# Seven products of quarters for layer 1's attention output, and layer 2 in three stages

## The chip, the cores and the metric

The kernel runs on one core of a Trainium2 chip. The metric is the device time in microseconds (us) of one execution; lower is better. The engines are named as the profile names them: PE is TensorE's matrix multiply and PEld its weight load, DVE is VectorE, ACT is ScalarE, POOL is GpSimd, and SP is SyncE, which here only issues DMA transfers. ACTq and SPq are the instruction streams of ACT and SP where they issue transfers.

## The reference

Four layers follow each other on `x` of shape (8, 512, 32, 32), all in float32. Two of them matter here.

```python
# layer 1: attention over the 1024 positions of an image
q, k, v = Wq x, Wk x, Wv x            # 64, 64 and 512 channels
scores = q^T k                        # (1024, 1024)
attn = softmax(scores, axis=-1)
out = v attn^T + x                    # 512 channels
# layer 2: add a bias, upsample by 2 with a 12-tap filter in both directions,
# leaky ReLU times sqrt(2), downsample by 2 with a 12-tap filter
```

Layer 0 is a group norm, an attention of eight heads, three steps `h + 0.1 tanh(W h)` and a projection, with a residual. Layer 3 is a conditional convolution block whose 1x1, 3x3 and 1x1 weights are mixed from eight experts by a router, with a residual.

## The kernel before

The eight images `b` are processed one after another through layers 0, 1 and 2; then layer 3 runs over all images. Each image's layer 2 result waits in DRAM (`spilled`) until then. The instructions are written with a tile framework: it gives every instruction to the queue of the engine that the code names, decides the order within each queue from its own estimates, places tiles in buffers and sets the semaphores. Each engine works its queue in order, so an instruction that waits holds up all that stand behind it.

SBUF holds seven `big` buffers of 128 x 4096 float32, taken by whatever tile is alive: `x` of this and the next image, `v`, the exponentials, halos, upsampled tiles, results. PSUM has three pools of two: `ps_sc` gives pairs of banks, `ps_tp` and `ps_mm` give single banks of 128 x 512.

Most 512 x 512 matrix products are already computed as seven products of quarters (the Strassen-Winograd scheme) in place of eight: `product`, whose matmuls all stand in L412, with `quarter_sums` making four sums of quarters of the data beforehand and callbacks named `made` that combine the products as they come out of PSUM. When a `product` has `rows=True` its matmuls have 256 columns, otherwise 512.

Layer 1 (`layer1`) for an image: queries and keys; `values`, the `v` of 1024 positions x 512 channels, as a `product`; between its steps, `scores(t)` computes transposed scores, and ACT their exponentials into `eT[0]` and `eT[1]` (L715), each 1024 keys by 512 of the queries; DVE adds them up into `accs` (L720, L722). `totals(sh)` turns `acc` into sums over the keys with 8 matmuls of one column (L729), and `inv` holds their reciprocals. Then comes a loop over eight row blocks `ic` of 128 positions:

```python
            for jc in range(SC):
                nc.tensor.matmul(
                    ps, eT[sh][:, jc, ts(u, P)], v[:, jc, :],
                    start=(jc == 0), stop=(jc == SC - 1),
                )
```

Each block is transposed (L756), gets a bias added (L758), is accumulated over eight key blocks of 512 channels (the lines above, L762), is multiplied by `inv` and added (L768), and its four image rows are written to a padded image in DRAM, `ypad`, by four transfers that ACT issues (L770). One block later SP issues the loads of a halo tile, `halo.load(t)`: four transfers of 9 x 14 pixels each (L796), which read back what the neighbouring blocks wrote. `midway` puts the next image's channel statistics (L277) in the middle of the loop.

Layer 2 first upsamples all eight tiles (`layer2_up`): for each tile four matmuls with a halo (L826), each followed by the leaky ReLU `leak`, ACT making 0.2 times the value (L810) and DVE the larger of the two (L811). Then it downsamples everything (`layer2_down`): three ranges of output rows, each from its own upsampled tiles, for each of four channel chunks (L857), evicted by ACT and DVE (L871 to L877). The next image's group norm follows.

On ACT's queue the square root of the next image's group norm (L294, with a table load) stands between the row writes of layer 1 and the first leak.

Of the kernel before, what the change touches and what calls it, by code (L numbers as in the profile page):

```python
# [17 lines left out]
P = 128  # L18
# [15 lines left out]
NT = 8  # L34
# [18 lines left out]
def tile_sequence(ctx: ExitStack, tc: tile.TileContext, a: dict, out: bass.AP, shifted: bool):  # L53
# [215 lines left out]

    def channel_stats(b, x):  # L270

        stats = work.tile([P, C], F32, tag="y", name=f"stats_{b}", bufs=2)
        stats = stats[:, 0 : CC * 2 * 6].rearrange("p (c h s) -> p c h s", c=CC, h=2)
        mv = small.tile([P, CC, 2], F32, tag="mv", bufs=2, name=f"mv_{b}")
        for cc in range(CC):
            for h in range(2):
                nc.vector.bn_stats(stats[:, cc, h, :], x[:, cc, ts(h, HALF)])  # L277
            nc.vector.bn_aggr(mv[:, cc, :], stats[:, cc, :, :].rearrange("p h s -> p (h s)"))
        return mv
# [387 lines left out]
    def layer1(b, x, w, midway):  # L667

        qk = big_tile(f"qk1_{b}", [P, S + HALF])
        q, k = qk[:, 0:S], qk[:, S : S + HALF].rearrange("d (p j) -> d p j", j=P)  # L670

        rows = [slice(HD * r, HD * r + HD) for r in range(2)]
        t_x = quarter_sums(f"x_{b}", x)
        for sh in range(2):
            ps = bank(ps_tp, name=f"qk1_{b}_{sh}")
            project(ps, w["qk1"], 0, x, sh)
            keys = ps[HD:P, :].rearrange("d (p r j) -> d p r j", r=2, j=P)
            for r in range(2):
                dst = k[rows[r], 2 * sh : 2 * sh + 2, :]
                if r == 0:  # L680
                    nc.vector.tensor_scalar_add(q[rows[r], ts(sh, HALF)], ps[0:HD, :], qk1_b[0:HD, :])
                    nc.vector.tensor_scalar_add(dst, keys[:, :, r, :], qk1_b[HD:P, :])
                else:
                    nc.scalar.activation(
                        q[rows[r], ts(sh, HALF)], ps[0:HD, :], AF.Identity, bias=qk1_b[0:HD, :]
                    )
                    nc.scalar.activation(
                        dst, keys[:, :, r, :], AF.Identity, bias=qk1_b[HD:P, :]
                    )
        shift = None  # L690
        if shifted:
            shift = big_tile(f"shift_{b}", [P, S])
            row_shifts(
                f"{b}", [q[rows[r], :] for r in range(2)],
                [qk[rows[r], S : S + HALF] for r in range(2)],
                [shift[HD * r : HD * r + 1, :] for r in range(2)],
            )
        v = big_tile(f"v1_{b}", [P, SC, C])
        eT = [big_tile(f"eT_{b}_{sh}", [P, SC, HALF]) for sh in range(2)]
        if b == 0:  # L700
            layer2_constants()
        inv = small.tile([P, SC], F32, tag="inv1", bufs=2, name=f"inv1_{b}")
        accs = {}

        def scores(t):
            sh, p = divmod(t, SC // 2)
            at = ts(sh, HALF)
            pool = (ps_tp, ps_mm)[t % 2]
            ps = [bank(pool, f"scores1_{b}_{t}_{r}") for r in range(2)]
            scores_T(  # L710
                ps, [k[rows[r], p, :] for r in range(2)], [q[rows[r], at] for r in range(2)],
                shift and [shift[HD * r : HD * r + 1, at] for r in range(2)],
            )
            for r in range(2):
                nc.scalar.activation(eT[sh][:, 2 * p + r, :], ps[r], AF.Exp)  # L715
            e = eT[sh][:, 2 * p : 2 * p + 2, :].rearrange("j r i -> j (r i)")
            if p == 1:
                accs[sh] = sums(f"acc1_{b}_{sh}")
                first = eT[sh][:, 0:2, :].rearrange("j r i -> j (r i)")
                nc.vector.tensor_add(accs[sh], first, e)  # L720
            elif p > 1:
                nc.vector.tensor_add(accs[sh], accs[sh], e)  # L722

        def totals(sh):
            acc = accs.pop(sh)
            ps = bank(ps_tp, f"total1_{b}_{sh}")
            for u in range(4):
                for r in range(2):
                    nc.tensor.matmul(  # L729
                        ps[:, u : u + 1], acc[:, r * HALF + u * P : r * HALF + u * P + P],  # L730
                        ones[:, 0:1], start=(r == 0), stop=(r == 1),
                    )
            at = slice(4 * sh, 4 * sh + 4)
            nc.vector.reciprocal(inv[:, at], ps[:, 0:4])
            for r in range(2):
                nc.gpsimd.tensor_add(seen, seen, acc[:, ts(r, HALF)])  # L736
            nc.gpsimd.tensor_add(seen[:, 0:4], seen[:, 0:4], inv[:, at])

        values = product(f"v1_{b}", w["v1"], x, t_x, positions(f"v1_{b}", v), rows=True)
        for _ in range(2):  # L740
            next(values)
        for steps in ((0,), (1, 2), (3, 4), (5, 6), (7,)):
            for t in steps:
                scores(t)
            next(values)
            if 4 in steps:
                totals(0)
        all_of(values)
        if b + 1 < B:
            w["v"] = weight("v", b + 1)  # L750

        halo = Halo(b)
        for ic in range(SC):
            ps = bank(ps_tp, f"xT_{b}_{ic}")
            for cc in range(CC):
                nc.tensor.transpose(ps[:, ts(cc, P)], x[:, cc, ts(ic, P)], ident)  # L756
            y = work.tile([P, C], F32, tag="y", name=f"y_{b}_{ic}", bufs=2)
            nc.vector.tensor_add(y, ps, row_bias)  # L758
            ps = bank(name=f"av1_{b}_{ic}")
            sh, u = divmod(ic, 4)  # L760
            for jc in range(SC):
                nc.tensor.matmul(  # L762
                    ps, eT[sh][:, jc, ts(u, P)], v[:, jc, :],
                    start=(jc == 0), stop=(jc == SC - 1),
                )
            if ic == 1:
                totals(1)
            nc.vector.scalar_tensor_tensor(y, ps, inv[:, ic : ic + 1], y, ALU.mult, ALU.add)  # L768
            for r in range(4):
                nc.scalar.dma_start(  # L770
                    ypad[b % 2][4 * ic + r + 3, 3 : W + 3, :], y[W * r : W * r + W, :]
                )
            if ic:
                halo.load(ic - 1)
            if ic == 3:
                midway()
        halo.load(NT - 1)
        halo.load_last()
        return halo

    class Halo:

# [19 lines left out]
        def load_last(self):  # L802
            self.read(self.last, H, 3, 3, W)

    def layer2_up(b, halo):
        up = []

        def leak(dst, ps, name):
# [1 line left out]
            nc.scalar.mul(t, ps, 0.2 * SQRT2)  # L810
            nc.vector.scalar_tensor_tensor(dst, ps, SQRT2, t, ALU.mult, ALU.max)  # L811

        for t in range(NT):
            if t % 2 == 0:
                two = big_tile(f"up_{b}_{t // 2}", [P, 8, C])
            up.append(two[:, 4 * (t % 2) : 4 * (t % 2) + 4, :])
            for c in (0, 2):

                n = 2 * t + c // 2
                if n % 3 == 2:  # L820
                    ps = [bank(name=f"up_{b}_{t}_{c + i}") for i in range(2)]
                else:
                    pair = ps_sc.tile([P, S], F32, tag="scores", name=f"up_{b}_{t}_{c}")
                    ps = [pair[:, ts(i, HALF)] for i in range(2)]
# [4 lines left out]
                    )  # L829
                for i in range(2):  # L830
                    leak(up[t][:, c + i, :], ps[i], f"{b}_{t}_{c + i}")
        ps = bank(name=f"up_{b}_63")[0 : 2 * W, :]
        nc.tensor.matmul(ps, up63_op[0 : 3 * W, :], halo.last, start=True, stop=True)
        up63 = tmp(f"up63_{b}")[0 : 2 * W, :]
        leak(up63, ps, f"{b}_63")

        return up, up63

    def layer2_down(b, up, up63, freed=lambda t: None):

        z = big_tile(f"z_{b}", [P, CC, S])
        for first, last, ts_ in ((0, 13, (0, 1, 2)), (9, 21, (3, 4)), (17, 31, (5, 6, 7))):
            for cc in range(CC):
                zr = z[:, cc, :].rearrange("p (h w) -> p h w", w=W)
                ps = bank(name=f"dn_{b}_{cc}_{first}")
# [26 lines left out]
                else:  # L875
# [3 lines left out]
                    if b + 1 < B:  # L879
                        nc.sync.dma_start(spilled[b][ts(cc, P), :], z[:, cc, :])  # L880
            freed(ts_[-1])
        return z

    with tc.tile_pool(name=f"weights_{run}", bufs=1) as wpool:
# [10 lines left out]
        for b in range(B):  # L895
# [10 lines left out]
            halo = layer1(b, x, w, midway)  # L906
            if not last:
                norm = norm_factors(b + 1, *stats)
                layer2_down(b, *layer2_up(b, halo))

# [85 lines left out]
                )  # L998
        return wt

    up, up63 = layer2_up(B - 1, halo)
    z_next = load_z(0)
    load_experts("w2_0", 3 * P)

    def freed(t):
        if t == 2:
            load_experts("w2_1", 3 * P)
        elif t == 4:
            load_experts("w2_2", 3 * P)
        else:  # L1010
            load_experts("w3", C)

    z_last = layer2_down(B - 1, up, up63, freed)
    wt_next = mixed(0)
    route(B - 1, B)
    for b in range(B):
# [126 lines left out]
```

## Time and profile before

Three runs took 4014.0 to 4014.68 us, median 4014.32. The profiled execution spans 4013.4 us.

| what | us busy | instructions |
|---|---|---|
| PE | 3931.3 | 13990 |
| DVE | 2416.2 | 3376 |
| ACT | 1092.8 | 1491 |
| POOL | 458.0 | 343 |
| PE, layer 1 exponentials by values (L762) | 450.1 | 1024 |
| PE, layer 2 upsampling (L826) | 233.0 | 512 |
| PE, layer 2 downsampling (L857) | 235.8 | 2048 |
| PE, layer 1 totals (L729) | 29.6 | 256 |
| DVE, leaky ReLU (L811) | 171.1 | 264 |
| ACT, leaky ReLU (L810) | 147.6 | 264 |

Every float32 matmul appears as two MATMUL records. A row of a timeline gives the start of a group of like instructions, the time to the end of its last, engine, line, operation, the tiles written and read, shapes and count; in square brackets stands the idle time before it and what ended that. A row of a table by stage gives the stretch, its length, and the busy time of PE, PEld, DVE, ACT and POOL with counts in brackets, then the granted TensorE clock, the share of the DMA engines that was busy, and GB/s. In a row of costliest groups stand busy time, mean ns of one, and after the bar the idle time of the engine before them.

### The profile page before, as it was taken

What the parts mean: (1) busy time and instruction counts of PE and PEld (TensorE: products, weight loads), DVE (VectorE), ACT (ScalarE), POOL (GpSimd) and SP (SyncE); (2) the same over time, 40 slices, a digit from 0 to 9 for tenths busy, and PEclk for the clock granted to TensorE, in tenths of its full rate; (3) what the DMA queues carried; (4) which work ended last, traced back from release to release, by engine and by line L of the source; (5) the groups of instructions that cost most, each with busy time, mean ns of one, the idle gap of its engine ahead of it and who ended that gap; (6) DMA issues with size and microseconds to landing.
All of it is one profiled execution on the core that took longest, in us unless ns stands there. A gap on an engine that the chain in (4) does not pass through costs nothing.

```text
span 4013.4 us, 36677 instructions
## 1 busy us (share of the span) xinstructions
PE 3931.3 (98%) x13990; PEld 1898.7 (47%) x13990; DVE 2416.2 (60%) x3376; ACT 1092.8 (27%) x1491; POOL 458.0 (11%) x343
## 2 busy tenths in 40 slices
PE   8999999999999999999999999999999999999998
PEld 4345543455435463355434564355634554345543
DVE  4777448634676437754586346764377445764885
ACT  1421224112332214212242124322142122321332
POOL 5320003000120003100030002200030001301000
PEclk9999999999999999999999999999999999999999
DMA  5002310131101420032101310023200221004432
GB/s 186 19 25 86 108 55 1 54 106 62 37 0 58 124 76 1 2 106 95 56 1 58 121 45 35 1 76 106 77 1 29 93 82 56 1 0 127 152 145 87
DMA packets 83546, 255.77 MB, mean 64 GB/s; under 512 B 13206, under 2 KB 19366, under 8 KB 76576
## 3 DMA queue, kind: packets, MB, share of 16 engines
q1 hardware_dynamic: 68368, 223.11, 15.7%
q10 hardware_dynamic: 12288, 16.79, 1.6%
q0 software_dynamic: 2704, 13.42, 0.9%
q8 instruction: 112, 1.84, 0.2%
q14 instruction: 74, 0.61, 0.0%
HBM read 192.47 MB, written 60.81 MB: 63 GB/s over the span
## 4 chain that ended last, share of the span: by engine, by line
PE 89%; DVE 7%; ACT 3%; issue 1%; DMA 0%; ACTq 0%; SPq 0%; DVEq 0%
PE scores L263 13%; PE av L626 11%; PE av L762 11%; PE inl_X L412 6%; PE dn L857 6%; PE v_X L412 4%; PE inl_Y L412 4%; PE inl_A L412 3%; PE c L1035 3%; DVE up L811 3%; PE v_Y L412 3%; PE proj_X L412 2%; PE k_X L412 2%; PE q_X L412 2%; PE v_A L412 2%; ACT leak L810 2%
## 5 line engine op out<-in xcount | busy, mean ns | idle before, releaser
L611 ACT ACTIVATE e<-scores 128x1024 f32<-128x1024 f32 x512 | 497.3, 1022 | 583.1 <-PE scores L263 583.0
L617 DVE TENSOR_TENSOR acc<-acc,e 128x1024 f32<-128x1024 f32 x384 | 494.1, 1287 | 122.9 <-ACT e L611 102.5
L263 PE MATMUL scores<-q,k 64*128 64x512 f32 x2048 | 511.0, 616 | 6.0 <-DVE v L493 3.3
L626 PE MATMUL av<-e,v 128*64 128x512 f32 x2048 | 494.1, 604 | 0.0
L762 PE MATMUL av<-v,eT 128*128 128x512 f32 x1024 | 450.1, 592 | 0.0
L643 POOL TENSOR_TENSOR seen<-seen,acc 128x512 f32<-128x512 f32 x128 | 213.5, 1668 | 1586.3 <-DVE acc L617 1581.3
L263 PEld LDWEIGHTS scores<-q,k 64*128 64x128 f32 x2048 | 175.8, 186 | 333.2 <-ACT e L611 162.1
L762 PEld LDWEIGHTS av<-v,eT 128*128 128x128 f32 x1024 | 189.6, 190 | 214.3 <-issue 212.1
L626 PEld LDWEIGHTS av<-e,v 128*64 128x64 f32 x2048 | 124.8, 136 | 338.8 <-issue 336.5
L826 PE MATMUL up<-halo,up_op 126*128 126x512 f32 x512 | 233.0, 604 | 12.8 <-DVE up L811 12.5
L857 PE MATMUL dn<-dn_op,up 128*128 128x126 f32 (+5 forms) x2048 | 235.8, 275 | 0.0
L857 PEld LDWEIGHTS dn<-dn_op,up 128*128 128x128 f32 (+1 forms) x2048 | 231.1, 192 | 8.7 <-DVE up L811 6.5
L768 DVE SCALAR_TENSOR_TENSOR y<-av,inv,y 128x512 f32<-128x512 f32 x64 | 48.0, 750 | 300.4 <-PE av L762 300.4
L640 DVE RECIPROCAL inv<-total 128x512 f32<-128x512 f32 x64 | 214.7, 3355 | 0.0
L811 DVE SCALAR_TENSOR_TENSOR up<-up,leak 128x512 f32<-128x512 f32 (+1 forms) x264 | 171.1, 685 | 62.2 <-ACT leak L810 56.6
L412 PE MATMUL inl_A<-hf,w_inl 128*128 128x512 f32 x384 | 178.0, 599 | 10.7 <-DVE hf L641 10.7
L412 PE MATMUL inl_X<-T_hf,w_inl 128*128 128x512 f32 x384 | 175.2, 592 | 0.0
L643 POOL TENSOR_TENSOR seen<-seen,inv 128x512 f32<-128x512 f32 x64 | 125.2, 1956 | 416.7 <-DVE inv L640 416.7
L810 ACT ACTIVATE leak<-up 128x512 f32<-128x512 f32 (+1 forms) x264 | 147.6, 594 | 88.3 <-DVE up L811 79.8
L826 PEld LDWEIGHTS up<-halo,up_op 126*128 126x128 f32 x512 | 91.9, 189 | 141.2 <-DVE up L811 74.3
L736 POOL TENSOR_TENSOR seen<-seen,acc 128x512 f32<-128x512 f32 x32 | 40.7, 1271 | 959.8 <-DVE acc L722 893.2
L506 ACT ACTIVATE inl_U<-inl_U,inl_b 128x512 f32<-128x512 f32 x96 | 66.7, 718 | 287.4 <-DVE inl_U L521 287.4
(273 smaller groups left out, 4986.9 us busy)
## 6 DMA issues: line engine op xcount, KB each, us to landing
halo<-ypad_u SPq DMA_DIRECT2D x256, 252.0 KB
w_v<-stored_u_v SPq DMA_DIRECT2D x14, 1792.0 KB
x<-in_x_dram SPq DMA_DIRECT2D x32, 512.0 KB
ypad_u<-y ACTq DMA_DIRECT2D x256, 64.0 KB
out_dram<-z SPq DMA_DIRECT2D x32, 512.0 KB
spill_u<-z SPq DMA_DIRECT2D x28, 512.0 KB
z<-spill_u SPq DMA_DIRECT2D x28, 512.0 KB
w_q<-stored_u_q SPq DMA_DIRECT2D x7, 1792.0 KB
```

Of the source, the lines that this page charges most:

```text
L263: nc.tensor.matmul(ps[r], k[r], q[r], start=True, stop=(shift is None))
L412: nc.tensor.matmul(dst, lhs, rhs, start=(opens and s == 0 and cc == 0), stop=(cc == 1 and s == rows), skip_group_check=True,)
L611: nc.scalar.activation(e, ps, AF.Exp, scale=HD ** -0.5)
L617: nc.vector.tensor_add(accs[g], accs[g], e)
L626: nc.tensor.matmul(avs[g][rows[r]], v[:, jc, ts(2 * oc + r, HD)], e[:, ts(r, HALF)], start=(jc == 0), stop=(jc == SC - 1),)
L640: nc.vector.reciprocal(inv, ps)
L643: nc.gpsimd.tensor_add(seen, seen, part)
L762: nc.tensor.matmul(ps, eT[sh][:, jc, ts(u, P)], v[:, jc, :], start=(jc == 0), stop=(jc == SC - 1),)
L810: nc.scalar.mul(t, ps, 0.2 * SQRT2)
L811: nc.vector.scalar_tensor_tensor(dst, ps, SQRT2, t, ALU.mult, ALU.max)
L826: nc.tensor.matmul(ps[i], up_op[0 : IR * IC, :], halo.tile(t)[0 : IR * IC, c + i, :], start=True, stop=True,)
L857: nc.tensor.matmul(rows[:, r0 - first : r1 + 1 - first, c0 : c1 + 1], up[t][0:k, c, ts(cc, P)], op[:, r0 - 4 * t + 3 : r1 + 4 - 4 * t, c0 ...
```

## The change

Layer 1's product of exponentials by values, 1024 x 1024 by 1024 x 512, is itself split into quarters and computed with seven products in place of eight (`weighted_rows`), to take an eighth of its matmul work away. The sums of quarters that this needs are made by DVE from the exponentials and from `v`: S1 to S4 of 512 x 512, T1 to T4 of 512 x 256. All matmuls now have 256 columns (L855 of the new kernel). A block of rows is complete only quarter by quarter: in the order C11, C12 (the upper rows), C22, C21 (the lower rows). So each image row is written by two transfers of half size (L765), and all transposes with the bias come first, into a big tile `y`.

The extra big tiles leave fewer buffers, so layer 2 is interleaved: upsample tiles 0 to 2, downsample the first range of rows, upsample 3 and 4, downsample the second, upsample 5 to 7, downsample the third. Its odd PSUM pairs come from `ps_tp` in place of `ps_mm`. In the last image the loads of the expert weights of layer 3 move to later points. `totals` first adds the halves of `acc` on DVE, so that four matmuls are enough, and the statistics take their scratch from the `sums` tiles.

```diff
         def totals(sh):
             acc = accs.pop(sh)
+            both = acc[:, 0:HALF]
+            nc.vector.tensor_add(both, both, acc[:, HALF:S])
             ps = bank(ps_tp, f"total1_{b}_{sh}")
             for u in range(4):
-                for r in range(2):
-                    nc.tensor.matmul(
-                        ps[:, u : u + 1], acc[:, r * HALF + u * P : r * HALF + u * P + P],
-                        ones[:, 0:1], start=(r == 0), stop=(r == 1),
-                    )
+                nc.tensor.matmul(
+                    ps[:, u : u + 1], both[:, ts(u, P)], ones[:, 0:1], start=True, stop=True
+                )
...
-        halo = Halo(b)
+        y = big_tile(f"y_{b}", [P, SC, C])
         for ic in range(SC):
             ps = bank(ps_tp, f"xT_{b}_{ic}")
             for cc in range(CC):
                 nc.tensor.transpose(ps[:, ts(cc, P)], x[:, cc, ts(ic, P)], ident)
-            y = work.tile([P, C], F32, tag="y", name=f"y_{b}_{ic}", bufs=2)
-            nc.vector.tensor_add(y, ps, row_bias)
...
+            nc.vector.tensor_add(y[:, ic, :], ps, row_bias)
+        totals(1)
...
+        def write(ic, cols):
             for r in range(4):
                 nc.scalar.dma_start(
-                    ypad[b % 2][4 * ic + r + 3, 3 : W + 3, :], y[W * r : W * r + W, :]
-                )
...
+                    ypad[b % 2][4 * ic + r + 3, 3 : W + 3, cols], y[W * r : W * r + W, ic, cols]
+                )
+        def written(what, u):
+            for ic in (2 * u, 2 * u + 1):
+                if what == "C11":
+                    write(ic, slice(0, QR))
+                elif what == "C12":
+                    write(ic, slice(QR, C))
+                elif what == "C22":
+                    write(ic + 4, slice(QR, C))
+                elif what == "C21":
+                    write(ic + 4, slice(0, QR))
+            if what == "C12":
+                for t in ((0,), (1, 2))[u]:
+                    halo.load(t)
...
+        weighted_rows(b, eT, v, inv, y, written)
+        for t in range(3, NT):
+            halo.load(t)
         halo.load_last()
...
+    def weighted_rows(b, eT, v, inv, y, written):
...
+        by_two(add, s1, a21, a22)
+        by_two(sub, t1, b12, b11)
+        by_two(sub, s2, s1, a11)
+        by_two(sub, t2, b22, t1)
+        by_two(sub, s3, a11, a21)
+        by_two(sub, t3, b22, b12)
+        for what, key, left, right in (
+            ("P1", "A", a11, b11), ("C11", "A", a12, b21), ("U2", "X", s2, t2),
+            ("W", "Y", s1, t1), ("C12", "Y", s4, b22), ("C22", "X", s3, t3),
+            ("C21", "X", a22, t4),
+        ):
+            for u in range(2):
+                ps = banks[key][u]
+                for s in range(2):
+                    for j in range(4):
...
+                made(what, u, ps)
+                written(what, u)
+            if what == "C11":
+                by_two(sub, s4, a12, s2)
+                by_two(sub, t4, b21, t2)
...
+        for t in range(3):
+            upsample(t)
+        z = big_tile(f"z_{b}", [P, CC, S])
+        downsample(0, 13, (0, 1, 2))
+        for t in (3, 4):
+            upsample(t)
+        downsample(9, 21, (3, 4))
+        for t in (5, 6, 7):
+            upsample(t)
```

In the changed program as built, the matmuls, sums and transfers of one image interleave more finely than the code is written: two of the first upsampling matmuls stand among C21's, and on ACT's queue all 64 row writes of an image stand in one run.

## The prediction

> **What bounds the kernel now.** First the page's busy shares and its chain of waits: TensorE is busy 98% of the span and carries 89% of the chain, at full clock throughout, so a change is worth the TensorE time that it removes, less the TensorE waits that it makes.
>
> ```profile
> PE 3931.3 (98%) x13990; PEld 1898.7 (47%) x13990; DVE 2416.2 (60%) x3376; ACT 1092.8 (27%) x1491; POOL 458.0 (11%) x343
> PE 89%; DVE 7%; ACT 3%; issue 1%; DMA 0%; ACTq 0%; SPq 0%; DVEq 0%
> L762 PE MATMUL av<-v,eT 128*128 128x512 f32 x1024 | 450.1, 592 | 0.0
> L826 PE MATMUL up<-halo,up_op 126*128 126x512 f32 x512 | 233.0, 604 | 12.8 <-DVE up L811 12.5
> ```
>
> Then TensorE's timeline of the second image around the change. In it a group's length overlaps the next group's start, so I take differences of starts.
>
> ```profile
> 543.16 7.07 PE L412 MATMUL v_A<-w_v,h 128*128 128x256 f32 x32
> 550.07 2.11 PE L412 MATMUL v_X<-w_v,T_h 128*128 128x256 f32 x9
> ...
> 845.24 0.60 PE L756 MATMUL xT<-ident,x 128*128 128x128 f32 x4
> 845.68 7.03 PE L762 MATMUL av<-v,eT 128*128 128x512 f32 x16
> 852.55 1.84 PE L729 MATMUL total<-ones,acc 128*128 128x1 f32 x16
> 854.25 0.63 PE L756 MATMUL xT<-ident,x 128*128 128x128 f32 x4
> ...
> 905.40 23.33 PE L826 MATMUL up<-halo,up_op 126*128 126x512 f32 x52 [1.52 <-DVE up L811]
> 929.23 1.07 PE L833 MATMUL up<-halo,up_op 96*64 96x512 f32 x2 [0.50 <-DVE up L811]
> ```
>
> A 512-column matmul is two records: 16 in 852.55-845.68 = 6.87 us, 0.4294 each. With 256 columns 32 take 550.07-543.16 = 6.91, 0.2159 each. The totals take 1.70. The same image by stage, exponentials by values, then upsampling, then downsampling:
>
> ```profile
> 837.93:898.12 60.19, 60.19 (x178) 29.28 (x177) 16.97 (x30) 0.00 (x0) 1.80 (x3) 1.00 0.51 157
> 898.12:930.23 32.11, 30.09 (x72) 12.12 (x70) 21.45 (x40) 18.87 (x33) 0.00 (x0) 1.00 0.30 92
> 930.23:960.98 30.75, 30.75 (x266) 30.06 (x265) 16.61 (x29) 4.48 (x9) 0.00 (x0) 1.00 0.13 52
> ```
>
> The first stage is all TensorE. The second has 66 upsampling records, 28.3 us, and two small ones, 0.3; it lasts 32.1, so it loses 3.5 us an image. ScalarE's timeline and VectorE's say why:
>
> ```profile
> 899.10 1.74 ACTq L770 DMA_DIRECT2D ypad_u<-y  x4
> 901.15 1.28 ACT L294 ACT_TABLE_LOAD   x1 [65.59 <-DMA ypad_u<-y]
> 902.45 0.26 ACT L294 ACTIVATE gmul<-gn_var,eps 128x4 f32<-128x4 f32 x1
> 902.61 0.59 ACT L810 ACTIVATE leak<-up 128x512 f32<-128x512 f32 x1
> 904.02 1.08 ACT L810 ACTIVATE leak<-up 128x512 f32<-128x512 f32 x2 [0.82 <-DVE gadd L299]
> ...
> 911.93 2.70 DVE L811 SCALAR_TENSOR_TENSOR up<-up,leak 128x512 f32<-128x512 f32 x4 [0.66 <-ACT leak L810]
> ```
>
> ScalarE issues the row writes itself, 0.43 us each and 0.475 from one to the next, and only then loads its table and starts the leaks. The first leak starts 4.5 us after the last av matmul; leaks then go at 6 in 5.3 us, and twelve take from 902.61 to about 914.0 = 11.4. The reader should keep this line of four writes in mind.
>
> **What the skill says.** "TensorE: Matmul & The Clock Gate", Back-to-back issue gap, gives 262 cycles for 256 columns and 518 for 512: half the columns cost half the time. The trace agrees (0.2159 against 0.4294), so a seventh product less is a real eighth. "DMA: Bandwidth & Descriptors", Issuing engines are not separate DMA queues, says that issues from several engines share the same 16 DMA engines; its Anatomy of one DMA says that a semaphore wait is served by the issuing sequencer before dispatch. The first agrees with DMA share 0.51 in the stage of writes and loads; of the second the trace of before has no clear case, since only four writes come at a time.
>
> **The change, part by part, per image.**
> Products: 64 blocks of 512 columns (128 records x 0.4294 = 55.0) become 7 x 16 of 256 (224 x 0.2159 = 48.4): -6.6 us. Both totals halved: half of 1.70 and of 1.77, -1.7; the added VectorE addition of 128x512 (0.68) ends before TensorE arrives, for the v1 product lies between. Together -8.3, or -66 us for eight images.
>
> VectorE gets 8 half quarters of S of 1024 (1.2 us each) and 8 of T of 512 (0.68), and more evictions (no row has 256 columns with two inputs; between 0.32 for 160 and 0.68 for 512, I take 0.4). From the first transpose to the end of C12's first half TensorE has 8 x 0.43 + 0.85 + 78 x 0.432 = 38 us; the queued VectorE work there, with the next image's statistics (5.6), adds to about 28. Walked in queue order, S2 and T2 are ready 13 us after the first transpose and first read at 19; S4 and T4 at 21, read at 35. Hidden behind P1, C11 and U2. Only the moved transposes wait, for two PSUM banks that VectorE drains between sums: +0.7 (0 to 2).
>
> Row writes: 64 of half size in place of 32. Each still has 32 rows, so I keep 0.475 an issue. After C11's and C12's first half 40 are left, and in the changed program's instruction order all stand on ScalarE ahead of the table load and every leak. Let T be TensorE's end of C12's first half. Rows are ready at T+1.2 (0.2 to start, 0.61, 0.4); 48 writes take 22.8, to T+24.0 at best. TensorE meanwhile needs 18 blocks for C22 and C12, 16 for C21, two upsampling matmuls: it ends C21 at T+17 (with 0.4 of wait for the first halo load, which I put at T+8.2: 5.1 us from row to last packet in before, and four more writes ahead of it, 1.9). ScalarE, idle in before, is now late.
>
> Semaphores: in the built order every DMA of both queues waits for one of eight semaphores in turn, so for the DMA eight before it. Twelve halo loads (tiles 0 to 2) stand among the writes of C12 and C22, and four of tile 3 among C21's. Loads land one per about 1.1 us (252 KB each; the packets of nine take 9.3 us in before) after T+8.2, the twelfth near T+20; the writes behind wait for it. Then 14 writes, 6.7, and again a wait for tile 3's loads: T+29 (24 to 32). Plus 0.3, 1.3 and 0.2: first leak at T+30.5.
>
> Three stages: the first upsampling stage has 12 leaks, 11.4 us, and 0.5 for the last blocks: T+42.4. TensorE can do between T+17 and there only ten upsampling matmuls (8.6) and 24 downsampling blocks (x 0.23 = 5.4), 14.0. Wait: 42.4-17-14.0 = 11.4 us. The second stage's leaks fit beside the downsampling; the third, where the normalisation (4 x 0.75 on VectorE) joins, +1.0. What the three stages win is before's 3.5, which is gone.
>
> Sum: -8.3 - 3.5 + 11.4 + 0.7 + 0.4 + 1.0 = +1.7 us an image, +14 for eight: 4028. The last image also loads its expert weights later; by their order they land before their mixing is needed: nothing, up to +3.
>
> **The rivals.**
> A: the semaphores cost nothing and only issuing counts. Leak at T+25.7, wait 6.6, -3.1 an image: 3989. For it: no DMA wait shows in before. Against: in before writes and loads never interleave.
> B: ScalarE's queue is never the limit (half-size writes are issued in half the time). Then the waits stay as in before, 3.5, and 66 us come off: 3948. Against: a 32-row write and a 126-row load are issued in 0.43 and 0.79 us, so time goes with rows, not bytes.
> C: writes and loads press on the DMA engines harder (each load 1.3 us among writes): ScalarE done at T+32, wait 14.6, +4.9 an image: 4053, and more if VectorE's sums delay a product.
>
> **How the numbers follow.** My forecast 0.50, A 0.24, B 0.10, C 0.16. Faster: B, nine tenths of A and a little of the forecast, 0.36; same: 0.14 from the forecast's and A's edges; slower: 0.50. The low end, 3975, lies below A and leaves out B; the high end, 4062, takes in C with 1.1 us an image more for the unknown VectorE costs.
>
> **What would show it.** Right: under the new L855 TensorE about 390 us of busy time; the row writes in one unbroken run on ScalarE's queue that ends over 10 us after C21's last matmul; TensorE idle 6 to 14 us an image, ended by VectorE's up; the table load behind a DMA. Wrong: leaks that start within 5 us of C21's end (B); TensorE idle inside L855, ended by VectorE (sums late); idle ended by a halo DMA.

## The result, and the profile after

The changed kernel takes 4078.22 us (median; 4076.54 to 4080.41), the kernel before beside it 4014.5: ratio 1.0159, 95% interval 1.0142 to 1.0177. It is slower by 64 us, 8.0 us an image; the forecast was slower by 14, 1.7 an image. The page of the changed kernel:

```profile
PE 3890.1 (95%) x14630; PEld 2042.5 (50%) x14630; DVE 2587.0 (63%) x3664; ACT 1103.6 (27%) x1507; POOL 444.8 (11%) x327
PE 87%; DMA 5%; DVE 5%; ACT 1%; issue 1%; ACTq 1%; SPq 0%; DVEq 0%
L913 PE MATMUL up<-halo,up_op 126*128 126x512 f32 x512 | 256.2, 636 | 99.5 <-ACT gmul L295 92.3
L934 PE MATMUL dn<-dn_op,up 128*128 128x126 f32 (+5 forms) x2048 | 248.8, 277 | 16.8 <-DVE up L898 16.1
```

TensorE is busy 41 us less (3931.3 before), yet its share fell from 98% to 95%. DMA, which carried 0% of the chain of waits, carries 5%, some 200 us of span. The upsampling row names the place: its idle time ahead of it went from 12.8 to 99.5 us, 92.3 of that ended by `gmul`, the square root that stands on ScalarE's queue between the row writes and the leaks. TensorE's timeline of the second image:

```profile
845.49 1.04 PE L757 MATMUL xT<-ident,x 128*128 128x128 f32 x8
...
880.92 3.72 PE L855 MATMUL av_Y<-v,eT 128*128 128x256 f32 x16
884.47 1.03 PE L855 MATMUL av_X<-v,eT 128*128 128x256 f32 x4
...
894.48 1.10 PE L913 MATMUL up<-halo,up_op 126*128 126x512 f32 x2 [1.76 <-DMA halo<-ypad_u]
...
903.40 2.93 PE L913 MATMUL up<-halo,up_op 126*128 126x512 f32 x6
920.20 2.08 PE L913 MATMUL up<-halo,up_op 126*128 126x512 f32 x2 [13.87 <-ACT gmul L295]
...
978.49 6.71 PE L413 MATMUL q_A<-h,w_q 128*128 128x512 f32 x15
```

The first half of C12 ends at 884.47, which is the T of the prediction; C21 ends at 903.40 = T+18.9 (forecast T+17). Then TensorE does three upsampling matmuls and waits 13.9 us. From the first transpose to the next image's `q_A` it is 133.00 us; before it was 960.98-837.93 = 123.05. ScalarE's timeline shows what is waited for:

```profile
885.92 32.64 ACTq L765 DMA_DIRECT2D ypad_u<-y  x48
918.59 1.28 ACT L295 ACT_TABLE_LOAD   x1 [60.47 <-DMA ypad_u<-y]
919.88 0.26 ACT L295 ACTIVATE gmul<-gn_var,eps 128x4 f32<-128x4 f32 x1
920.04 0.59 ACT L897 ACTIVATE leak<-up 128x512 f32<-128x512 f32 x1
```

Before, this run had four writes (899.10, 1.74 us) and the first leak came 4.5 us after the last av matmul. Now it has 48, takes 32.64 us, and the first leak comes at T+35.6, 16.6 us after C21. At 0.475 an issue 48 writes are 22.8 us; the other 9.8 are waits inside the run. The forecast had T+30.5.

### The profile page after: what moved, and what is told of

Read it like the earlier page. It is cut to its first block, busy times and chain, and to the rows that moved or that the text cites. A ratio compares the mean times of both kernels' runs of the same rounds, so it can differ in the third digit from the quotient of the medians.

```text
span 4074.7 us, 38294 instructions
## 1 busy us (share of the span) xinstructions
PE 3890.1 (95%) x14630; PEld 2042.5 (50%) x14630; DVE 2587.0 (63%) x3664; ACT 1103.6 (27%) x1507; POOL 444.8 (11%) x327
## 4 chain that ended last, share of the span: by engine, by line
PE 87%; DMA 5%; DVE 5%; ACT 1%; issue 1%; ACTq 1%; SPq 0%; DVEq 0%
PE scores L263 13%; PE av L627 11%; PE inl_X L413 6%; PE dn L934 6%; PE up L913 5%; PE v_X L413 4%; PE inl_Y L413 4%; PE inl_A L413 3%; DMA halo<-ypad_u 3%; PE c L1129 3%; PE v_Y L413 3%; PE av_Y L855 2%; PE av_A L855 2%; PE proj_X L413 2%; PE q_X L413 2%; PE k_X L413 2%
## 5 line engine op out<-in xcount | busy, mean ns | idle before, releaser
L644 POOL TENSOR_TENSOR seen<-seen,acc 128x512 f32<-128x512 f32 x128 | 213.6, 1669 | 1681.7 <-DVE acc L618 1676.7
L913 PE MATMUL up<-halo,up_op 126*128 126x512 f32 x512 | 256.2, 636 | 99.5 <-ACT gmul L295 92.3
L934 PEld LDWEIGHTS dn<-dn_op,up 128*128 128x128 f32 (+1 forms) x2048 | 246.6, 194 | 67.5 <-issue 31.6
L934 PE MATMUL dn<-dn_op,up 128*128 128x126 f32 (+5 forms) x2048 | 248.8, 277 | 16.8 <-DVE up L898 16.1
L913 PEld LDWEIGHTS up<-halo,up_op 126*128 126x128 f32 x512 | 95.2, 200 | 193.2 <-ACT gmul L295 98.1
L616 DVE TENSOR_TENSOR acc<-e,e 128x1024 f32<-128x1024 f32 x64 | 82.9, 1295 | 102.5 <-ACT e L612 102.5
L518 DVE TENSOR_TENSOR inl_U<-inl_X,inl_P 128x512 f32<-128x512 f32 x96 | 61.9, 686 | 111.4 <-PE inl_X L413 111.4
L736 POOL TENSOR_TENSOR seen<-seen,acc 128x512 f32<-128x512 f32 x16 | 22.5, 1408 | 976.7 <-DVE acc L728 905.4
L413 PEld LDWEIGHTS inl_A<-hf,w_inl 128*128 128x128 f32 x384 | 70.4, 190 | 110.2 <-issue 95.4
```

Source lines behind the costliest of these rows:

```text
L413: nc.tensor.matmul(dst, lhs, rhs, start=(opens and s == 0 and cc == 0), stop=(cc == 1 and s == rows), skip_group_check=True,)
L644: nc.gpsimd.tensor_add(seen, seen, part)
L913: nc.tensor.matmul(ps[i], up_op[0 : IR * IC, :], halo.tile(t)[0 : IR * IC, c + i, :], start=True, stop=True,)
L934: nc.tensor.matmul(rows[:, r0 - first : r1 + 1 - first, c0 : c1 + 1], up[t][0:k, c, ts(cc, P)], op[:, r0 - 4 * t + 3 : r1 + 4 - 4 * t, c0 ...
```

## The experiments

All times are medians, against the kernel before on the same chip (4014.5 to 4015.2). They come in four groups: the parts alone, the row writes, a second wait behind the first, and TensorE's clock. Where an edit adds or takes away lines, the line numbers of its run shift by a few (L909 or L912 for L913).

### The parts alone

The halved totals, put into the kernel before (the first hunk of the change, nothing else):

> The kernel before with the halved totals alone (both totals: one VectorE addition and four small matmuls in place of eight). Theory: 8 x 1.7 us are saved, since TensorE has no slack there: 4001, 3998 to 4005. Rival (the added VectorE addition of 0.68 us is waited for, or the small matmuls overlap others): 4011 to 4016.

Measured: 3998.68 (ratio 0.9960, 0.9947 to 0.9974), 15.9 us less, a little more than the 13.6 forecast. TensorE's waits are as before: none took the place of the removed matmuls.

The kernel before with the totals and with layer 2 in three stages (with the banks and the later loads of the last image that belong to them), its av matmuls and row writes left as they were; the line that calls them:

```diff
-                layer2_down(b, *layer2_up(b, halo))
+                layer2(b, halo)
```

> The kernel before with the halved totals and layer 2 in three stages, but with its own products and row writes of 512 columns after each row block. Theory (three stages turn before's 3.5 us of TensorE waits in upsampling into a wait of 1 to 3 us for the first twelve leaks): 0 to 2.5 us an image less than with the totals alone, 3979 to 3999. Rival (the three stages themselves make the long wait, by asking for leaks earlier): over 4010.

Measured: 3981.69 (0.9917, 0.9900 to 0.9933), another 17.0 us: 1.6 us in each of the first seven images, and about 5 in the last, where the loads moved too. So three stages do not make a wait by themselves: two of the change's three parts together are 33 us faster than the kernel before, and what turns that into 64 slower is the new product with its row writes. The opposite cut, the changed kernel without three stages:

```diff
-        for t in range(3):
+        for t in range(NT):
             upsample(t)
...
         downsample(0, 13, (0, 1, 2))
-        for t in (3, 4):
-            upsample(t)
         downsample(9, 21, (3, 4))
-        for t in (5, 6, 7):
-            upsample(t)
...
         downsample(17, 31, (5, 6, 7))
```

> The changed kernel with all upsampling ahead of all downsampling, as before the change. Theory: 33 leaks at 0.95 us follow one another from 35.6 us after C12's first half, TensorE idles through them, then 30.75 us of downsampling: 97.7 us after it in place of 94.0, so 3 to 5 us an image more, 4100 to 4118. Rival (the three stages make the long wait): at most 4078.

Measured: 4077.77, no difference from the changed kernel. The expectation missed. The number is the rival's, but the three stages do not make the wait: without them TensorE still waits 11.8 us at layer 2's start in the second image, ended by `gmul`. From the first leak (921.23) to the next `q_A` (979.54) of the second image this kernel takes 58.3 us, the changed one 978.49-920.04 = 58.4, where I had worked out 33 x 0.95 + 30.75 = 62.1: some downsampling goes between the leaks here too. Where leaks start this late, the three stages gain nothing.

### The row writes

The writes moved to another queue:

```diff
         def write(ic, cols):
             for r in range(4):
-                nc.scalar.dma_start(
+                nc.sync.dma_start(
```

> The 64 row writes an image are issued on SyncE's queue instead of ScalarE's; all else as in the changed kernel. Theory (ScalarE's queue of writes holds the table load and the leaks back): the first leak no longer starts 35.6 us after C12's first half but within about 3 us of C21's end or of the landing of the first three tiles, TensorE's idle at layer 2's start falls from 14 to under 4 us an image, 11 to 16 us an image are saved: 3950 to 3990. Rival (the transfers are late whoever issues them: 24 writes at 0.475 and 12 loads at 0.83 on one queue still take over 21 us): the idle stays over 8 us, now ended by a halo DMA, and the time stays over 4030.

Measured: 4045.19 (1.0073, 1.0058 to 1.0088), 33 us better than the changed kernel, and short of the 88 to 128 expected. In its second image C21 ends at 899.70. ScalarE's first leak, and VectorE's half of the eighth and ninth leak:

```profile
900.82 0.60 ACT L897 ACTIVATE leak<-up 128x512 f32<-128x512 f32 x1 [5.07 <-PE up L913]
```

```profile
908.54 0.69 DVE L898 SCALAR_TENSOR_TENSOR up<-up,leak 128x512 f32<-128x512 f32 x1 [0.67 <-ACT leak L897]
919.52 0.69 DVE L898 SCALAR_TENSOR_TENSOR up<-up,leak 128x512 f32<-128x512 f32 x1 [10.29 <-DMA ypad_u<-y]
```

The first half of the theory holds: with the writes off its queue ScalarE starts 1.1 us after C21 instead of 16.6. Then VectorE stops at the ninth leak for 10.3 us, behind a row write. The ninth leak is the first of tile 2; its output `up_1` is a big tile of its own, and it was placed in the buffer of `y`, which is free only when the last row write has read it. In the other images the trace names a halo load as the end of this wait (64.6 us in six of them); on SyncE's queue writes and loads use the same eight semaphores in turn. The prediction had not seen this second wait.

The same bytes in half as many writes, on ScalarE's queue:

```diff
-                if what == "C11":
-                    write(ic, slice(0, QR))
-                elif what == "C12":
-                    write(ic, slice(QR, C))
+                if what == "C12":
+                    write(ic, slice(0, C))
...
                 elif what == "C21":
-                    write(ic + 4, slice(0, QR))
+                    write(ic + 4, slice(0, C))
```

> Each image row is written once with all its 512 columns, upper rows after C12 and lower rows after C21: 32 writes an image of 64 KB in place of 64 of 32 KB, the same bytes, on ScalarE's queue as in the changed kernel. Theory (the number of issues counts, not the bytes): the last write is issued about 24 to 30 us after C12's first half instead of 34, the first leak comes 4 to 8 us earlier, 32 to 64 us in all: 4014 to 4046. Rival (bytes or landings count): an issue takes twice as long and the time stays within 10 us of 4078.

Measured: 4033.91 (1.0049, 1.0034 to 1.0064), 44 us better. C12's first half ends at 883.00 in its second image and the table load starts at 910.56, so T+27.6 instead of T+34.1:

```profile
884.44 26.09 ACTq L765 DMA_DIRECT2D ypad_u<-y  x32
```

An issue of 32 rows takes the median 0.43 us whether a row has 1 KB or 2: the number of issues counts. Sixteen fewer are 7.6 us; the waits inside the run stay, 26.09 - 32 x 0.475 = 10.9 us. The Trainium skill agrees: "DMA: Bandwidth & Descriptors", Rules for kernel authors, says to coalesce many small transfers.

The halo loads of tiles 0 to 3 taken off the eight semaphores that they share with the writes:

```diff
-            nc.sync.dma_start(dst, pixels)
+            queue = nc.gpsimd if row <= 12 else nc.sync
+            queue.dma_start(dst, pixels)
```

> The halo loads of tiles 0 to 3 are issued on GpSimd's queue instead of SyncE's; the writes stay on ScalarE's queue. In the built order the writes then no longer share their eight semaphores with those loads. Theory (9.8 us of the 32.6 us run of writes are waits for loads that stand eight places before): the run of the last 48 writes shrinks to about 23 to 25 us, the first leak comes 8 us earlier, 40 to 70 us less: 4008 to 4038, unless GpSimd issues the loads so slowly that TensorE waits for them instead. Rival (the writes are slow because the DMA engines are busy): the run stays near 32 us and the time at 4078 or more.

Measured: 4059.01 (1.0106, 1.0090 to 1.0121), 19 us better; 40 to 70 were expected. The end of C12's first half (TensorE's timeline, the start of the group after it) and the table load (ScalarE's):

```profile
886.79 1.03 PE L855 MATMUL av_X<-v,eT 128*128 128x256 f32 x4
```

```profile
917.97 1.28 ACT L295 ACT_TABLE_LOAD   x1 [57.53 <-DMA ypad_u<-y]
```

That is T+31.2. Of the 9.8 us of waits in the run, taking these loads off the shared semaphores saves about 3. The other 7 remain when a write waits only for earlier writes: the write itself lands late. The DMA engines are busy 0.72 to 0.96 of the time around 912 to 920 in the changed kernel. In both kernels the writes follow each other without a gap until the loads have begun (loads from 890.78 and first gap over 0.1 us at 894.13 in the changed kernel, 893.59 and 898.25 here). That landing is slow because of the loads is my reading; no run here took the loads away.

### The second wait

To free the ninth leak from `y`'s buffer I issue the loads of tiles 6 and 7 after the first upsampling stage, so that their buffer takes the place of `y`:

```diff
-        for t in range(3, NT):
+        for t in range(3, 6):
             halo.load(t)
-        halo.load_last()
...
+        for t in (6, 7):
+            halo.load(t)
+        halo.load_last()
         downsample(0, 13, (0, 1, 2))
```

With the writes of quarter rows on SyncE's queue:

> e1_sp (64 writes of quarter rows an image on SyncE's queue) with the halo loads of tiles 6 and 7 issued after the first upsampling stage, which lets their buffer, and not the output of the ninth leak, take the place of y. Theory (the second wait is for y's buffer, that is for the landing of the last row write): VectorE's wait of 10.3 us ahead of the ninth leak is gone; 6 to 10 us an image less than e1_sp, 3965 to 3997. Rival (that wait is for the halo tile or for the DMA engines): it stays, and the time is within 10 us of 4045.

Measured: 3985.16 (0.9926, 0.9911 to 0.9941), 60 us less than e1_sp. The edit also takes loads out of the first stage, so a rival is that the row writes now land earlier. SyncE's writes after C21, which ends at 889.93 in this run's second image, and VectorE's half of the eighth and ninth leak:

```profile
893.57 16.20 SPq L765 DMA_DIRECT2D ypad_u<-y  x31
```

```profile
898.77 1.29 DVE L897 SCALAR_TENSOR_TENSOR up<-up,leak 128x512 f32<-128x512 f32 x2 [0.66 <-ACT leak L896]
```

The last write is issued at 909.77, 19.8 us after C21 (18.6 in e1_sp), and the ninth leak is done 10 us before that. The writes are as late as ever and the leak no longer waits for them: the buffer was the wait. In the built programs `up_1` has the place of `y` in the changed kernel, e1_sp, e5_full_sp and e6_full_pool; in e9_sp_late the halo of tiles 6 and 7 has it, in e10_pool_late `z`. The same edit alone on the changed kernel:

> The changed kernel with the halo loads of tiles 6 and 7 issued after the first upsampling stage and nothing else: the output of the ninth leak no longer takes y's buffer. Theory (in the changed kernel the second wait lies inside the first: when ScalarE starts its leaks it has issued every write, and the last has landed before the ninth leak): no gain, 4070 to 4085. Rival (the buffer is a wait of its own there too): 3990 to 4050.

Measured: 4076.34. There the second wait lies inside the first, and taking it away is worth nothing. Each cause hides the other: e1_sp alone gives 33 us, e14_late alone 2, both 93.

Now with full-width writes, on SyncE's queue without and with the late loads:

> Full-width writes (32 an image, as in e2_full) and these on SyncE's queue (as in e1_sp). Theory (two things hold the first upsampling stage: ScalarE's queue of writes ahead of the leaks, and, seen in e1_sp, the ninth leak, whose output takes the buffer of y and waits until the last row write has landed): the last write is issued about 26 us after C12's first half instead of 34, the first leaks start right after C21, the ninth waits 0 to 4 us, TensorE's idle at layer 2's start is 0 to 5 us an image: 3950 to 3990, below the kernel before. Rival (the halo transfers themselves hold the stage once the writes do not): idle of 6 us or more ended by a halo DMA, 4000 or more.

> e5_full_sp with the late loads of tiles 6 and 7. Theory: 3.4 us of wait ahead of the ninth leak gone: 3960 to 3980. Rival (later loads waited for in the third stage): 3995 or more.

Measured: 3995.17 (0.9948, 0.9931 to 0.9964) and 3949.11 (0.9837, 0.9822 to 0.9852). Both miss their ranges, the first above, the second below: a wait of 3.4 us at VectorE's ninth leak costs about 6 us an image (46 us in eight); I put that down to the downsampling of all four channel chunks, which stands behind tile 2. And with the lower rows' writes on GpSimd's queue, the upper rows' on ScalarE's:

```diff
         def write(ic, cols):
+            queue = nc.scalar if ic < 4 else nc.gpsimd
             for r in range(4):
-                nc.scalar.dma_start(
+                queue.dma_start(
```

> Full-width writes, the upper rows' on ScalarE's queue and the lower rows' on GpSimd's. Theory: no write stands behind a halo load any more, the lower rows' writes are issued within 6 us of C21's end, so that the ninth leak does not wait: 3940 to 3980. Rival (GpSimd issues slowly or its transfers land late): the ninth leak or the halo load of tile 3 waits for the last row write, 3990 to 4030.

> e6_full_pool with the late loads of tiles 6 and 7, as in e9_sp_late. Theory: the ninth leak's wait of 3.2 us is gone and TensorE's 2.5 us idle with it: 3950 to 3970, the fastest so far. Rival (the later loads are waited for in the third stage): 3984 or more.

Measured: 3983.82 (0.9923, 0.9907 to 0.9940), just above its range, since the ninth leak still waited 3.2 us in the second image, and with the late loads 3947.35 (0.9833, 0.9818 to 0.9848), a little below the expected range and the fastest kernel of the study, 67 us below the kernel before. The chain of waits of its page, and its second image on TensorE and on ScalarE:

```profile
PE 93%; DVE 5%; ACT 1%; issue 1%; DMA 0%; SPq 0%; DVEq 0%; ACTq 0%
```

```profile
830.61 1.04 PE L757 MATMUL xT<-ident,x 128*128 128x128 f32 x8
...
886.61 4.65 PE L909 MATMUL up<-halo,up_op 126*128 126x512 f32 x10
891.09 0.56 PE L930 MATMUL dn<-dn_op,up 112*128 112x66 f32 x4
...
946.27 7.13 PE L413 MATMUL q_A<-h,w_q 128*128 128x512 f32 x16
```

```profile
871.05 9.38 ACTq L766 DMA_DIRECT2D ypad_u<-y  x16
880.46 1.28 ACT L295 ACT_TABLE_LOAD   x1 [37.21 <-DMA halo<-ypad_u]
...
887.73 0.60 ACT L893 ACTIVATE leak<-up 128x512 f32<-128x512 f32 x1 [5.08 <-PE up L909]
```

Sixteen writes instead of 48 stand ahead of the table load, which is done before C21 ends (886.61). TensorE goes from C21 into layer 2 with no bracket of idle time, DMA is at 0% of the chain, and the image takes 115.66 us from the first transpose to `q_A`. The skill's "DMA: Bandwidth & Descriptors", Issuing engines are not separate DMA queues, says that issuing from several engines saves only the sequencer's time, usually small beside the transfer. Here this time was not small: 48 writes held ScalarE's queue for 32.64 us, 22.8 of them issuing, the rest waiting between issues. Not all of it was lost, since most of it ran beside TensorE's product. In the changed kernel the first leak starts 16.6 us after C21, in e1_sp 1.1; of these 15.5 us the waits inside the run are 9.8, and the issuing is about 5.7.

### TensorE's clock

The mean granted clock fell from 0.998 to 0.983. The changed kernel by small stretches, around the wait of the second image (after the busy times come the granted clock, the DMA share and GB/s):

```profile
907.00:910.00 3.00, 0.00 (x0) 0.00 (x0) 0.00 (x0) 0.00 (x0) 0.00 (x0) 1.00 0.49 153
910.00:911.00 1.00, 0.00 (x0) 0.00 (x0) 0.00 (x0) 0.00 (x0) 0.00 (x0) 0.84 0.26 67
911.00:920.00 9.00, 0.00 (x0) 0.00 (x0) 0.00 (x0) 1.40 (x2) 0.00 (x0) 0.50 0.78 239
920.00:923.00 3.00, 2.80 (x6) 1.55 (x6) 2.00 (x7) 1.72 (x4) 0.00 (x0) 0.50 0.87 265
...
925.00:926.00 1.00, 1.00 (x7) 0.71 (x6) 0.87 (x2) 0.92 (x2) 0.00 (x0) 1.00 0.88 264
```

The clock halves about 4.4 us into the idle time (it began at 906.33) and is full again some 4 us after work resumes at 920.20; two records at 920.20 take 1.87 us instead of 0.86. "TensorE: Matmul & The Clock Gate", What's actually happening, describes this: half rate after at least one idle window of about 3.4 us, full rate after about as long a busy one. Does it cost anything here? Matmuls put into the wait should keep the clock up; their result is unread:

```diff
         halo = Halo(b)
+        halo.y = y
...
+                if t == 0 and c == 2:
+                    warm = bank(name=f"warm_{b}")
+                    for _ in range(13):
+                        nc.tensor.matmul(
+                            warm, up_op[0 : IR * IC, :], halo.y[0 : IR * IC, 7, :],
+                            start=True, stop=True,
+                        )
```

> The changed kernel with 30 matmuls of 512 columns into an unused bank of PSUM, issued by TensorE in its wait at layer 2's start (30 x 0.43 = 12.9 us of the 13.9), their result unread. In the changed kernel the granted clock falls to 0.50 about 4.5 us into that wait and is back about 4 us after it. Theory A (the halved clock costs nothing, since the leaks on ScalarE and VectorE set the pace of that stage at 0.95 us each): the clock stays at 1.00 in the records and the time is 4076 to 4086, the plus for downsampling blocks that come later. Theory B (the halved clock costs the 2 us an image by which those matmuls are longer): 4060 to 4066.

> The changed kernel with 26 matmuls of 512 columns into an unused bank of PSUM, all between C21 and the upsampling matmul that waits (26 x 0.43 = 11.2 us of the 13.9; what is left is under 4 us), their result unread; in e7_warm most of them had stood behind the wait. Theory A (the halved clock costs nothing, since the leaks set the pace of that stage): mean granted clock above 0.99 and the time 4074 to 4086, the plus for four downsampling blocks that come later. Theory B (the halved clock costs 2 us an image): 4058 to 4070.

These two, with 30 and 26 matmuls, took 4209.97 and 4125.55 and tell nothing on the question: I had priced a 512-column matmul at one record of 0.43 us, while it takes two, so that 26 of them are 22.3 us and overran the wait; in e7_warm most also stood behind it. With 13:

> As e12_warm26 with 13 matmuls of 512 columns: 13 x 0.86 = 11.2 us of the 13.9 us wait, so that under 4 us of idle are left. Theory A (the halved clock costs nothing, since the leaks set the pace of that stage): mean granted clock above 0.99 in the records and a time of 4074 to 4086, the plus for downsampling blocks that come later. Theory B (the halved clock costs about 2 us an image): 4058 to 4070.

Measured: 4085.15 (1.0173, 1.0159 to 1.0187), mean clock 0.993. The matmuls and TensorE's next work, then stretches by clock:

```profile
909.01 11.32 PE L911 MATMUL warm<-y,up_op 126*128 126x512 f32 x26
922.27 1.12 PE L921 MATMUL up<-halo,up_op 126*128 126x512 f32 x2 [1.93 <-ACT gmul L295]
```

```profile
913.00:920.00 7.00, 7.00 (x18) 2.92 (x16) 0.00 (x0) 0.00 (x0) 0.00 (x0) 1.00 0.68 204
924.00:926.00 2.00, 0.92 (x2) 0.51 (x3) 1.29 (x2) 1.13 (x3) 0.00 (x0) 0.86 0.82 281
```

The clock stays at 1.00 through the wait, and the time is no lower. But the run does not decide between the theories, because the clock is halved right after: in this image from 925.4 to 928.9, while TensorE works, and so in five of the seven images that another image follows. The way from the first leak to the next `q_A`, image by image, says more:

| kernel | clock after the first leak | images | first leak to `q_A`, us |
|---|---|---|---|
| changed | halved until 3.7 to 4.3 us after it | 1, 2, 6 | 58.1 to 58.4 |
| changed | halved until 6.0 to 6.9 us after it | 3, 4, 5, 7 | 59.3 to 59.7 |
| e13_warm13 | 1.00 | 1, 3 | 58.4 to 58.5 |
| e13_warm13 | halved for 3.4 or 6.8 us | 2, 4, 5, 6, 7 | 59.7 to 61.1 |
| e10_pool_late | 1.00 | 2 to 7 | 58.2 to 58.6 |

(In the first image of e10_pool_late the first leak stands ahead of C21's end, so that it can't be compared.) In three images of the changed kernel the halved clock costs nothing that can be seen, as theory A says: the twelve leaks of the first stage take 11.2 us in the second image and 11.3 in that of e10_pool_late. In the other four a longer halving goes with about 1 us an image, some 4 to 5 us in all, out of a loss of 131; that it is the cause is not shown. Theory B's 2 us in every image is not what the changed kernel shows.

## Why the prediction was wrong in size

The forecast's direction, slower, and the place were right; the size was too small by 50 us. The runs split the +64 into the forecast's own terms:

| term | forecast, us | measured, us | from |
|---|---|---|---|
| both totals halved | 8 x -1.7 = -14 | -15.9 | e4_totals against before |
| before's 3.5 gone, third stage +1.0 | 8 x -2.5 = -20 | -17.0 | e8_three against e4_totals |
| seven products, transposes' wait | 8 x (-6.6 + 0.7) = -47 | -34.3 | e10_pool_late against e8_three |
| wait at layer 2's start, first halo load | 8 x (11.4 + 0.4) = +94 | +130.9 | changed kernel against e10_pool_late |
| sum | +14 | +63.7 | |

- The products: in the second image the way from the first transpose to `q_A` is 115.66 us in e10_pool_late and 121.42 in e8_three, 5.8 less against 5.9 forecast. In total they give 13 us less than forecast, mostly because the first and the last image gain little: the same way in the first image is 119.5 us against 121.1, and from the last image's first transpose to the end it is 372.8 us in e10_pool_late and 372.2 in e8_three. The forecast multiplied one image by eight. The row is a difference of two kernels and holds their other small waits too (1.3 and 6.0 us before upsampling matmuls in all).
- VectorE's sums were hidden, as forecast: in the second image no idle time of TensorE inside L855 is ended by VectorE. In the first image 3.6 us are, where TensorE waits for VectorE to combine products, and 1.2 in the last: the sign of being wrong that the forecast named, in small. The busy time of L855, summed over its five groups, is 415 us against "about 390", which I had worked out from starts, while busy times overlap.
- The step that failed is the size of the wait at layer 2's start, 37 us too small in the sum. The mechanism was the forecast one: the writes in one run on ScalarE's queue, ending 15 us after C21, the table load behind a DMA, the leaks behind that. But "ACT writes end T+29" was T+34.1. I had put the waits inside the run at 5 us, all from halo loads on shared semaphores; they are 9.8, and with the loads on other semaphores (e3_sem) only about 3 go away. A write that waits for the eighth before it waits for a landing, and I had priced landings from a trace in which only four writes ever stood together. The first leak moved from T+30.5 to T+35.6, 5.1 us an image, some 40 us in all; C21 also ended 1.9 us later than forecast, 1.4 of that in the wait for the first halo load (1.76 against 0.4).
- The last image: forecast 0 to +3 for later expert loads. From its first transpose to the end it takes 387.1 us in the changed kernel against 380.5 before, with the same wait at layer 2's start (16.1 us, ended there by VectorE's `up`). The expert loads themselves are not seen in a wait. A load of `z` that moved with them ends a wait of 4.2 us of VectorE, after which TensorE does not wait.
- Rival C, with loads pressing on the DMA engines and ScalarE done at T+32, was nearest (4053), and right in that landings are slow. Rival A's unbroken issuing (T+24) and rival B were wrong for the kernel as built; B's time, 3948, is what e10_pool_late and e11_full_sp_late reach once the writes no longer hold the leaks, but by another sum: B counted 66 us for totals and products and kept before's waits; the runs give 50 for these, and 17 for the three stages. That the two agree is chance.
- The forecast said that TensorE's idle time would be ended by VectorE's `up`. It is ended by ScalarE's square root: the next upsampling matmul takes a bank of `ps_tp`, and the trace names `gmul`, which reads the variance from that pool, as the one who frees it.
- Not in the forecast at all: the wait of the ninth leak for `y`'s buffer. It costs nothing in the changed kernel (e14_late), but any mending of the first wait runs into it (e1_sp, e5_full_sp, e6_full_pool).

## What to carry to other kernels

When a change multiplies small transfers, count the issues, add the waits of the run for its own landings, and ask what else stands on the queue that issues them; halving their number, moving them and freeing the buffer behind them was worth 131 us here, the eighth product that was saved 34. Before mending a wait, look for the next one behind it: a tile that takes the buffer of a tile still being written out waits for the last transfer (10.3 us in e1_sp). With two waits one inside the other, removing the inner one alone gives nothing and the outer one alone only a part. And price waits on landings from the crowded stage to come, not from the empty one of before. A probe that is to keep a state, as the clock here, has to be read after the place where it acts, too.

## What the runs showed of the hardware

A TensorE clock that was halved in a wait of 12 to 14 us and stayed so for 3.7 to 4.3 us of the leaks after it cost nothing that can be seen (58.1 to 58.4 us from first leak to `q_A`, against 58.2 to 58.6 at full clock in e10_pool_late); where it stayed so for 6.0 to 6.9 us, the same way took 59.3 to 59.7. Row writes of 32 rows took 0.42 to 0.43 us to issue on ScalarE's and on SyncE's queue, with rows of 1 KB and of 2 KB alike, and 0.50 on GpSimd's.
